# How the rows of three expert tiles reach TensorE: whole rows turned by TensorE, or blocks of 32 by 32 turned by VectorE

## The chip, the core and the metric

The kernel runs on one core of a Trainium2 chip. TensorE (PE) multiplies matrices into PSUM, VectorE (DVE) and ScalarE (ACT) do elementwise work, GpSimd (POOL) issues indirect DMAs here, and SyncE (SP) issues most of the other DMAs, one after the other. The metric is the device time of one execution in microseconds, as the median of several runs.

## The reference

A graph-attention layer over 4096 nodes is followed by a mixture of experts. The second part is the one that matters here: each row is normed, a gate picks two of eight experts for it, and each expert is a two-layer network with a GELU between.

```python
x = x + gnn(_layernorm(x), adj, ...)              # attention over 4096 nodes, 4 heads
top_w, top_i = jax.lax.top_k(xf @ Wg + bg, 2)     # xf: layer-normed rows, 4096 x 256
top_w = jax.nn.softmax(top_w, axis=-1)
for e in range(8):                                # W1[e]: 256 x 1024, W2[e]: 1024 x 256
    h = gelu(xf @ W1[e] + b1[e])
    out = out + w_dense[:, e:e + 1] * (h @ W2[e] + b2[e])
```

## The kernel before, in words

The attention takes the rows in four ranges of 1024. While a range is attended to, the rows of the range before it are finished, routed, and written with their gate weights into one list per expert in device memory (`lists`, 260 floats a row). The experts then work on tiles of 256 rows of one list. There are 17 such tiles that can be planned before the last rows are routed (9 `early`, 8 `mid`), then 8 `final` tiles, one for each expert, of 512 rows or fewer, and 2 of the kind `rest`.

The last range of the attention ends at about 777 us. From there the loop at L2027 goes over the tiles: `up` multiplies a tile with W1 and sends it through the GELU on ScalarE (L1885, L1889), `turn` brings the next tile's rows into the form that `up` needs, with the 256 features on the partitions (`xT`), and `down` multiplies with W2 (L1919). Its results are scaled by VectorE (L1932, into `o`) and added to the output by GpSimd (L1944). TensorE works in the order in which the code is written here (`order_of`), so what `turn` puts on TensorE stands between `up` of a tile and `down` of the same tile. VectorE, ScalarE and SyncE take the work in an order that the scheduler lays down at build time.

Between the parts of the first tiles, `between(n)` puts the last 1024 rows of the attention: their results are turned back (L1551), normed and summed on VectorE (L1554 to L1584, two halves of 512 rows with one Newton root of six short steps and more in each, L168 to L181), turned for the gate (L1257, copied out of PSUM by ScalarE at L1260), and routed (L1268 to L1349). The tiles share PSUM with this work: all turned pieces go through three rotating banks of the name `bank`.

A tile's rows come in one of two ways, which `fetch` (L1789) chooses by `NEAR`:

- Of the first `NEAR` tiles the whole rows are loaded by one DMA of 260 KB (`load_rows_of`, L575, into `early`; the first tile into `xr0` ahead of this stage). `turn_rows_of` (L607) turns each by four transposes of 128 by 128 on TensorE (L611, into `pt`) and two copies on ScalarE (L613), or one on ScalarE and one on VectorE (L615).
- Of the later tiles the rows are loaded in blocks (`load_blocks_of`, L583): one small DMA for the four values behind each row (`known`, L588), and eight DMAs of 32 partitions by 8 blocks by 32 floats (`xr`, L595), which put each block of 32 by 32 where it belongs in the turned tile. One VectorE instruction then turns every block in place (L1869).

After the rows, `fetch` asks for the second bias, W1 and W2 of the tile (L1804, L604, L1811). Each has two buffers, and so the DMA waits until the tile two before is done with its own. Three tiles are fetched ahead of the loop, and each pass of it fetches one more. The whole rows of tiles 2 to 6 are asked for in this prologue:

```python
        for i in range(1, NEAR):
            load_full(i)
            if i in (1, 4):
                jobs.append(fetch(*todo[len(jobs)]))
            if i in (1, 2):
                given.append(loads_of(b0 + i - 1, (residuals, large)[i - 1]))
```

Tiles are counted from 1 in the text; the code counts `i` from 0.

Of the kernel before, what the change touches and what calls it, by code (L numbers as in the profile page):

```python
# [44 lines left out]
def gat_then_moe(  # L45
# [34 lines left out]
    MID = BOTH - EARLY  # L80
    LATE = 2 * N // TT - BOTH
    SURE = 2
    NEAR = 6
    KT = -(-N // TT)
    LAG = 6

# [132 lines left out]
    def forward(apart, stack):  # L219
# [352 lines left out]
        def load_rows_of(t, i, xr):  # L572
            rows = TT
            first = entry(t, 1, i, E * LIST - WT)
            ins = nc.sync.dma_start(  # L575
                xr, lists[bass.ds(first, rows), :].rearrange("(c p) d -> p c d", p=CH)
            ).ins
            needs_of(ins, False)
# [40 lines left out]
        with ExitStack() as layer:  # L619
# [893 lines left out]
            def loads_of(b, room):  # L1513

                xb, rb = loaded("xf"), room("rb")
                nc.sync.dma_start(rb, rows_of(residual, b))
                nc.sync.dma_start(xb, rows_of(x, b))
                return xb, rb
# [270 lines left out]
        def fetch(t, i):  # L1789

            rows = rows_of_job(t, i)
            nch = -(-rows // CH)
            chosen = t is early or t is mid
            near = chosen and i + EARLY * (t is mid) < NEAR
            if near:
                xr = full_rows[i]
                known = xr[:, :, D:]
            else:
                xr = work.tile([P, DC, rows // Q, Q], F32, tag="xr", name="xr")
                known = work.tile([CH, nch, RW - D], F32, tag="known", name="known")  # L1800
                load_blocks_of(t, i, xr, known, chosen)
            e = entry(t, 0, i, E - 1)
            b2b = work.tile([CH, D], F32, tag="b2b", name="b2b")
            nc.sync.dma_start(b2b, b2[bass.ds(e, 1)].to_broadcast([CH, D]))  # L1804
            if t is early and i == 0:
                w1 = w10
            else:
                w1 = work.tile([P, DC, F], F32, tag="w1", name="w1")
                load_first(t, i, w1)
            w2 = work.tile([P, FC, D], F32, tag="w2", name="w2")  # L1810
            nc.sync.dma_start(w2, W2[bass.ds(e, 1)].rearrange("o (c p) d -> p (o c) d", p=P))  # L1811
            job = {"t": t, "i": i, "xr": xr, "known": known, "w1": w1, "w2": w2, "nch": nch, "b2b": b2b}
            job["rows"], job["near"] = rows, near
            job["last"] = t is rest and i == SURE - 1

            job["into"] = out[: N - R] if t is early or t is mid else out
            return job
# [196 lines left out]
        def load_full(i):  # L2014
            xr = work.tile([CH, 2, RW], F32, tag="early", name="early", bufs=NEAR - 1)
            load_rows_of(early, i, xr)
            full_rows.append(xr)

        for i in range(1, NEAR):
            load_full(i)  # L2020
            if i in (1, 4):
                jobs.append(fetch(*todo[len(jobs)]))
            if i in (1, 2):
                given.append(loads_of(b0 + i - 1, (residuals, large)[i - 1]))
# [61 lines left out]


    held, further, held_back, last_sums = forward(True, ctx)
    with tc.If(held(1, 1) > 0):
        further()  # L2090
        with tc.If(held(2, 1) > 0):
            with ExitStack() as again:
                held, further, rest_of_sums, _ = forward(False, again)
                with tc.If(held(1, 1) > 0):
                    further()
                for add in rest_of_sums:
                    add()
            for o in last_sums:
                nc.gpsimd.memset(o, 0.0)
# [31 lines left out]
```

## Time and profile before

| what | value |
|---|---|
| median of three runs | 1255.57 us (1255.51 to 1255.64) |
| the profiled execution's own time | 1254.18 us |
| its span, first to last instruction | 1252.5 us |
| granted TensorE clock | 0.999 |
| TensorE matmuls busy | 1237.9 us, 99% of the span |
| VectorE busy | 845.1 us, 67% |
| ScalarE busy | 448.2 us, 36% |
| DMA share from 801 to 841 us | 0.62 of the 16 engines |
| DMA share from 843 to 1000 us | 0.92 of the 16 engines |

Times within the execution are counted from the start of the span. A line of the chain of waits has the start, the duration and the piece of work that the end of the program hung on. A line of the timeline has the start, the busy time, the engine, the source line, the operation, what it wrote and read, and in brackets how long the engine stood idle before and what ended that. The DMA share is the mean busy share of the 16 DMA engines.

### The profile page before, as it was taken

To read this page: it belongs to the slowest core of one execution; us is meant where nothing else is said; L and a number is where in the kernel's file an instruction comes from. 1 tells how busy PE (TensorE), PEld (TensorE's weight loads), DVE (VectorE), ACT (ScalarE), POOL (GpSimd) and SP (SyncE) were. 2 spreads that over 40 slices of the span, in tenths; PEclk is the share of its full clock that TensorE was granted. 3 is DMA by queue.
4 is the path that set the end of the run, shared out by engine and by line. 5 is a ranking of instruction groups with operands and counts; after the bars stand their busy time and mean duration, and the time that the engine had idled before them with its cause. 6 is when DMAs were issued, how large, how long until landed. Compare 5 with 4: busy or idle time off the path is not lost.

```text
span 1252.5 us, 22714 instructions
## 1 busy us (share of the span) xinstructions
PE 1237.9 (99%) x8872; PEld 647.5 (52%) x8872; DVE 845.1 (67%) x1566; ACT 448.2 (36%) x918; POOL 241.8 (19%) x217
## 2 busy tenths in 40 slices
PE   9999999999999999999999999999999999999997
PEld 5444444332233332332324423888888876666686
DVE  7998887879999989999999996855111211111110
ACT  4332322165522375322645321533323332222322
POOL 4000000001002601006110015124432222222222
PEclk9999999999999999999999999999999999999999
DMA  6333433436533746334366422868999895455662
GB/s 216 118 119 111 164 114 102 150 121 133 187 105 102 236 114 206 103 102 153 113 159 200 128 81 91 273 169 217 229 251 252 222 230 119 106 137 112 135 163 32
DMA packets 155540, 190.22 MB, mean 152 GB/s; under 512 B 72312, under 2 KB 125680, under 8 KB 155040
## 3 DMA queue, kind: packets, MB, share of 16 engines
q1 hardware_dynamic: 133392, 145.39, 40.1%
q0 software_dynamic: 20544, 36.74, 13.3%
q10 hardware_dynamic: 1488, 6.55, 1.5%
q8 instruction: 71, 1.16, 0.4%
q14 instruction: 45, 0.37, 0.1%
HBM read 155.77 MB, written 29.74 MB: 148 GB/s over the span
## 4 chain that ended last, share of the span: by engine, by line
PE 94%; DVE 3%; issue 1%; ACT 1%; DMA 0%; POOLq 0%; SPq 0%; DVEq 0%; ACTq 0%
PE acc L1202 33%; PE po L1919 18%; PE ph L1885 17%; PE den L1211 17%; PE pr L1057 2%; DVE w L1701 2%; PE ph L1105 2%; PE ptx L1257 0%; DMA early<-lists 0%; PE acc L898 0%; PE pt L784 0%; PE ptr L1503 0%; PE po L1958 0%; PE pl L1268 0%; PE acc L748 0%
## 5 line engine op out<-in xcount | busy, mean ns | idle before, releaser
L1202 PE MATMUL acc<-w,ha 128*32 128x512 f32 x4096 | 669.9, 593 | 1.3 <-ACT u L1413 0.9
L1701 DVE SCALAR_TENSOR_TENSOR w<-er,eb,am 128x1024 f32<-128x1024 f32 x496 | 606.0, 1275 | 31.1 <-PE den L1211 30.9
L1211 PE MATMUL den<-w,unit 128*2 128x512 f32 x2048 | 467.0, 592 | 0.1
L1202 PEld LDWEIGHTS acc<-w,ha 128*32 128x32 f32 x4096 | 184.9, 110 | 292.4 <-issue 253.7
L1618 ACT ACTIVATE am<-adj 128x1024 bf16<-128x1024 int32 x124 | 130.7, 1054 | 346.2 <-DVE w L1701 211.7
L1885 PE MATMUL ph<-xT,w 128*128 128x256 f32 (+5 forms) x864 | 229.9, 423 | 0.2 <-ACT hT L1889 0.2
L1919 PE MATMUL po<-w,hT 128*128 128x256 f32 (+1 forms) x1040 | 229.7, 379 | 0.0
L1889 ACT ACTIVATE hT<-ph,bias 128x256 f32<-128x256 f32 (+5 forms) x216 | 111.1, 517 | 288.1 <-issue 186.2
L1919 PEld LDWEIGHTS po<-w,hT 128*128 128x128 f32 (+1 forms) x1040 | 195.7, 189 | 31.2 <-issue 3.1
L1885 PEld LDWEIGHTS ph<-xT,w 128*128 128x128 f32 x864 | 163.5, 190 | 59.7 <-issue 38.0
L1932 DVE SCALAR_TENSOR_TENSOR o<-po,share,b2s 128x256 f32<-128x256 f32 (+2 forms) x66 | 31.5, 478 | 210.9 <-PE po L1919 182.8
L1211 PEld LDWEIGHTS den<-w,unit 128*2 128x2 f32 x2048 | 93.7, 85 | 148.1 <-issue 139.7
L1944 POOL DMA_INDIRECT out<-o,ids x66 | 102.6, 1554 | 323.3 <-DMA out<-o,ids 141.5
L1388 POOL DMA_INDIRECT lists<-xe,at x64 | 89.3, 1395 | 267.6 <-issue 184.2
L1869 DVE STREAM_TRANSPOSE xT<-xr 128x512 f32<-128x512 f32 (+5 forms) x21 | 17.9, 851 | 70.9 <-PE ph L1885 31.2
L1057 PE MATMUL pr<-wr,xT 128*128 128x256 f32 x128 | 30.4, 381 | 0.2 <-ACT er L1151 0.2
L1907 ACT ACTIVATE b2s<-b2b,share 128x256 f32<-128x256 f32 x68 | 30.0, 499 | 0.0
L1125 POOL DMA_DIRECT2D residual<-rb x6 | 4.7, 784 | 121.2 <-DVE rb L1072 121.2
L1453 POOL DMA_DIRECT2D xf<-in_x x6 | 8.1, 1345 | 102.2 <-ACT xf L1452 102.2
L1057 PEld LDWEIGHTS pr<-wr,xT 128*128 128x128 f32 x128 | 24.1, 190 | 5.4 <-issue 0.9
L1105 PE MATMUL ph<-wall,xT 128*128 128x264 f32 x96 | 24.6, 399 | 0.0
L207 ACT ACTIVATE m<-y,off 128x256 f32<-128x256 f32 x48 | 23.7, 494 | 1.1 <-DVE off L215 0.6
(394 smaller groups left out, 616.4 us busy)
## 6 DMA issues: line engine op xcount, KB each, us to landing
adj<-in_adj SPq DMA_DIRECT2D x126, 512.0 KB
w<-in_L_ffn_W SPq DMA_DIRECT2D x54, 1024.0 KB
er<-parts ACTq DMA_DIRECT2D x3, 2048.0 KB
lists<-zeros POOLq DMA_DIRECT2D x8, 520.0 KB
residual<-rb POOLq DMA_DIRECT2D x8, 512.0 KB
rb<-residual SPq DMA_DIRECT2D x8, 512.0 KB
out<-y POOLq DMA_DIRECT2D x8, 512.0 KB
xb<-in_x SPq DMA_DIRECT2D x7, 512.0 KB
```

Of the source, the lines that this page charges most:

```text
L1057: order_of(nc.tensor.matmul(pr[:, k, :], turned[b][:, c, ts(t0 + k, P)], wr[:, c, :], start=(c == 0), stop=(c == DC - 1),))
L1105: order_of(nc.tensor.matmul(phs[t - t0], xT[:, c, ts(t, P)], wall[:, c, :], start=(c == 0), stop=(c == DC - 1),))
L1202: queue(nc.tensor.matmul(acc[half][h // 2][here : here + Q, :], ha[:, j, h * K + g * Q : h * K + (g + 1) * Q], w[half][h], start=(j == 0), ...
L1211: queue(nc.tensor.matmul(den[here : here + HB, :], unit[:, j, h, 1 - half : 1 - half + HB], w[half][h], start=(j == 0 and half == 0), stop ...
L1388: ins = nc.gpsimd.indirect_dma_start(lists, bass.IndirectOffsetOnAxis(ap=at[:, k, t : t + 1], axis=0), xe[:, t, :], None,).ins
L1618: nc.scalar.activation(am, at, AF.Relu, scale=2.0)
L1701: marks["w"] = nc.vector.scalar_tensor_tensor(wh[:, these], er[:, these, h], eb[:, j, h : h + 1], mask[:, these], op0=OP.max, op1=OP.min,).ins
L1885: order_of(nc.tensor.matmul(ph, job["w1"][:, c, ts(f, P)], xT[:, c, :], start=(c == 0), stop=(c == DC - 1),))
L1889: job["gelu"] = nc.scalar.activation(hT[:, f, :], ph, AF.Gelu, bias=job["bias"][:, f : f + 1]).ins
L1919: order_of(nc.tensor.matmul(po[:size], hT[:, f, k * CH : k * CH + size], w2[:, f, :], start=(f == 0), stop=(f == FC - 1),))
L1932: given_out.append(nc.vector.scalar_tensor_tensor(o[:size], po[:size], share[:size, k : k + 1], b2s[k][:size], op0=OP.mult, op1=OP.add,).ins)
L1944: added.append(add().ins)
```

## The change

`NEAR` goes from 6 to 3, and the number 4 in the prologue becomes `NEAR - 1`, which is 2.

```diff
-    NEAR = 6
+    NEAR = 3
...
         for i in range(1, NEAR):
             load_full(i)
-            if i in (1, 4):
+            if i in (1, NEAR - 1):
                 jobs.append(fetch(*todo[len(jobs)]))
             if i in (1, 2):
                 given.append(loads_of(b0 + i - 1, (residuals, large)[i - 1]))
```

Through `NEAR`, tiles 4, 5 and 6 are loaded by `load_blocks_of` and turned at L1869. The buffers `early` go from five to two (`bufs=NEAR - 1`). Tile 3 is now fetched after two whole-row loads instead of four.

## The prediction, made before the changed kernel had run

> **What bounds the kernel now.** I read the shares by engine first, then the chain of waits in order of time through the expert tiles, then each engine's timeline where the change lies. The page's first part and the head of the chain:
>
> ```profile
> PE 1237.9 (99%) x8872; PEld 647.5 (52%) x8872; DVE 845.1 (67%) x1566; ACT 448.2 (36%) x918; POOL 241.8 (19%) x217
> PE 94%; DVE 3%; issue 1%; ACT 1%; DMA 0%; POOLq 0%; SPq 0%; DVEq 0%; ACTq 0%
> ```
>
> TensorE sets the end. So only time that TensorE spends or loses between about 777 us and the end counts, and what it wins there arrives at the end if nothing later makes it wait. The chain where tiles 4, 5 and 6 are turned:
>
> ```profile
> 818.46 0.48 ACT xT L1260
> 818.94 0.04 issue
> 818.98 0.44 PE pt L611 x2
> ...
> 850.69 0.44 PE pt L611 x4
> 851.12 6.91 PE po L1919 x32
> ...
> 865.15 6.91 PE po L1919 x32
> 872.06 6.91 PE ph L1885 x32
> ```
>
> For tile 4 the second pair of transposes waited for a PSUM bank which ScalarE was still copying out. Tile 6 shows the transposes without the wait. Tile 7, the first loaded in blocks, has nothing between two runs of 6.91 us; from there TensorE's own list of waits is empty to 1245 us. TensorE's timeline gives the price of one turn (start, busy time):
>
> ```profile
> 818.26 0.38 PE L611 MATMUL pt<-ident,early 128*128 128x128 f32 x2
> 818.98 0.44 PE L611 MATMUL pt<-ident,early 128*128 128x128 f32 x2 [0.34 <-ACT xT L1260]
> ...
> 834.83 0.38 PE L611 MATMUL pt<-ident,early 128*128 128x128 f32 x2
> 835.45 0.44 PE L611 MATMUL pt<-ident,early 128*128 128x128 f32 x2 [0.24 <-ACT xT L1260]
> 835.72 7.07 PE L1919 MATMUL po<-w,hT 128*128 128x256 f32 x32
> ...
> 850.52 0.60 PE L611 MATMUL pt<-ident,early 128*128 128x128 f32 x4
> 850.96 7.07 PE L1919 MATMUL po<-w,hT 128*128 128x256 f32 x32
> ```
>
> The first `po` of tile 3 starts at 819.26, so the three turns hold TensorE for 1.00, 0.89 and 0.44 us.
>
> [...] L1869 writes `xT` itself in 0.71 us, while L611 needs a copy (L613). [...] a 128 B packet of `xr` held its engine 15.1 ns on average, a 1040 B packet of `early` 50.3 ns, so a byte is 2.4 times as dear in blocks. [...] the trace shows L1869 held 7.30 us at 959.37.
>
> **The change, part by part.**
>
> *Removed from TensorE*: three times four transposes. At a pitch of 0.109 us that is 1.31 us, and with the bank waits behind ScalarE, 1.00 + 0.89 + 0.44 = 2.33 us. The built order of the changed kernel has exactly these twelve gone, with `down` directly after the gate's transposes. What is late next: `down` needs a PSUM room (of the two, the earlier was given back by 808.0 us, before 818.3), its W2 (asked for at 794.4) and the first GELUs (the last ends at 818.06, and is needed 1.5 us after `down` starts). Nothing else stands there, so I take the full 2.33.
>
> *Removed from ScalarE*: six copies, 3 x 0.65 = 2 us, off the path.
>
> *Added on VectorE*: three turns of 0.71 us, 2.1 us. VectorE is full up to 826 us, so they push what is behind. The built order puts the first after a root step of the first half (806.44 to 806.60), ahead of `xe`, and moves the second half's `y` (L1563) ahead of `xe` too:
>
> ```profile
> 807.94 1.52 DVE L1584 TENSOR_SCALAR xe<-y,mv,r 128x256 f32<-128x256 f32 x4
> ```
>
> `xe` then ends at 809.46 + 0.71 + 1.22 = 811.4. TensorE wants it at 817.38, so 6.0 us cover it. The second half's `xe` has two turns and one scaling (0.48) more ahead of it: 825.50 + 1.90 = 827.4, wanted at 833.96 - 1.00, so 5.6 us. The third turn lies behind the routing step that TensorE waits for. Price: 0; without the cover, each microsecond costs one.
>
> *Moved on SyncE*: five whole-row loads become two, and 27 block loads come in: 24 DMAs more. Nine take 6.56 us of the queue (843.74 to 850.30):
>
> ```profile
> 843.74 0.37 SPq L588 DMA_DIRECT2D known<-lists  x1
> 844.30 6.00 SPq L595 DMA_DIRECT2D xr<-lists  x8
> ...
> 853.79 0.71 DVE L1869 STREAM_TRANSPOSE xT<-xr 128x512 f32<-128x512 f32 x1 [0.16 <-issue]
> ```
>
> In the built order those of tile 4 follow W2 of tile 3, which waits for `down` of tile 1 (issued 794.36). So they go out from 795.3 to 801.9, and SyncE was idle from 795.8 to 803.0. Landing took 2.3 to 4.8 us after the last issue where VectorE stood waiting (912.97, 959.37), so the blocks are there at 804.2 to 806.7, and VectorE asks at 806.6. Those of tiles 5 and 6 fall into 811.6 to 818.2 and 826.3 to 832.9, where SyncE also sat idle until 820.4 and 836.95. Behind them stand bias, W1 and W2 of the same tile: W1 of tile 4 went out at 803.9, and `up` wants it at 825.9. Price 0. Two loads that disappear stood ahead of tile 3's weights, which go out up to 2.7 us earlier, also covered.
>
> *DMA engines*: a tile in blocks is 2048 packets x 15.1 ns and 256 small ones x 9.2 ns, over 16 engines 2.1 us; in rows 256 x 50.3 ns, 0.8 us. Three tiles add 3.9 us, against 0.38 x 40 = 15 us idle from 801 to 841. Price 0.
>
> *Later on*: TensorE runs 2.33 us ahead into the stretch from 843 us where the engines are 0.92 busy. The tightest place in it is the scaling held behind a late turn: 946.55 against the next use of that room at 951.5. Of 4.9 us, 2.6 remain. Turned tiles themselves were at least 8.7 us early.
>
> **Sum.** Span 1252.5 - 2.33 = 1250.2; the profiled execution 1254.18 - 2.33 = 1251.85. It ran 1.39 us under the median, so the median becomes 1255.57 - 2.33 = 1253.2 us. That is 0.19%, just inside the 0.2% (2.5 us) that a measurement of this kernel can tell from no change.
>
> **Rivals.**
>
> *B, the bank waits come back.* Only the 1.31 us of transposes are won if the 1.0 us of waiting moves to the next user of a bank: 1254.3. For it: ScalarE still copies the gate's two turned pieces. Against: the next bank (`pl`) is asked for 6.9 us later.
>
> *C, more is won.* At 785.23 VectorE had waited 0.89 us for the whole rows of tile 2, and TensorE stood behind it. With three such loads gone from the queue around it, up to 0.9 us could come back: down to 1252.4. Against: those loads stand behind the rows of tile 2 in the same queue.
>
> *D, VectorE takes the bound.* If tile 4's blocks land late, L1869 holds `xe`, and TensorE stops at 817 us. This costs from a landing after 812.6 on, eats the gain at 814.9, and from 817.4 on shows as slower. For it: the worst tile of the trace took 15.0 us from its first block DMA to its turn (930.46 to 945.47), which would be 810.3 here, and W2 of tile 3 is in flight in front of them. Against: that was with the engines full, here they are 0.62 busy. Landing 5 us past 814.9 would give 1258.2.
>
> *E, the late stretch swallows it.* If the added packets put the turns more than 2.6 us later there, TensorE waits and part of the gain goes: about 1254.5. Against: shares of 0.59 and 0.63 at 852 and 868 us let the queue empty.
>
> **Chances and range.** The forecast 0.56, of which 0.22 lies past 2.5 us, since a turn's cost is known only to 0.1 to 0.2 us; its own range is 1252.9 to 1253.7. B 0.08, C 0.20, D 0.12 (0.11 slower by over 0.2%), E 0.04. Faster 0.22 + 0.20 = 0.42, slower 0.11, same the rest, 0.47. From 1252.3 to 1255.2 leaves out D and a little of C.
>
> **What would show it.** Right: no L611 after 805 us; `po` of tile 3 directly behind `ptx`, 1.0 us earlier; `up` of tile 6 starting at 855.8 instead of 858.1; TensorE without waits to the end; L1869 near 807, 824 and 837. Wrong: an idle time of TensorE before `ptx` at 817 or 833 put down to VectorE (D), a wait at `pl` or `ptx` for ScalarE (B), `po` waiting for L1932 after 900 us (E), or tile 2's transposes earlier than 786.2 (C).

## The result, and the profile after

The changed kernel took 1252.77 us (median of 17 runs, 1251.38 to 1257.34), the kernel before 1255.49 us in the same set (17 runs, 1253.96 to 1258.76). The ratio is 0.9983 with a 95% interval of 0.9975 to 0.9991, so 1.1 to 3.1 us less. The forecast was 1253.2 us, from 2.33 us of TensorE time.

The kernels here have execution times in two groups about 1.5 us apart (before: near 1254.0 and near 1255.5; changed: 1251.4 to 1251.8 with a mean granted clock of 0.998 to 0.999, and 1252.7 to 1253.5 with 0.997), and a median can fall in either group, so below each run also has a length out of its trace. It goes from the start of tile 2's `up` to the start of tile 6's `up` and covers all three turns. The profiled execution of the changed kernel (1253.52 us, span 1251.7 us, clock 0.997) had TensorE at half its clock for 3.4 us, from 7.8 to 11.3 us, ahead of that length; the one of before has its clock at 1.00 there. Behind the stretch, at L1148, it was 1.40 us later than before (15.32 us against 13.92). Its stage begins 1.38 us later, and the times below are shifted by that much.

| from tile 2's `up` to tile 6's `up` | before | after |
|---|---|---|
| start of `up` of tile 2 | 794.16 us | 795.54 us |
| start of `up` of tile 6 | 858.00 us | 857.05 us |
| length | 63.84 us | 61.51 us |

That is 2.33 us less, to the last digit what the three turns had held. TensorE's timeline of the kernel before has the two starts, and the gate's transposes (`ptx`) and `po` around the turn of tile 4:

```profile
794.16 2.75 PE L1885 MATMUL ph<-xT,w 128*128 128x256 f32 x12
...
817.38 1.04 PE L1257 MATMUL ptx<-ident,xe 128*128 128x128 f32 x8
...
819.26 7.07 PE L1919 MATMUL po<-w,hT 128*128 128x256 f32 x32
...
858.00 7.15 PE L1885 MATMUL ph<-xT,w 128*128 128x256 f32 x32
```

The shares by engine on the page of the changed kernel, first:

```profile
PE 1237.3 (99%) x8860; PEld 646.3 (52%) x8860; DVE 846.9 (68%) x1569; ACT 446.8 (36%) x912; POOL 241.9 (19%) x217
```

Twelve matmuls and six ScalarE instructions are gone; VectorE has three instructions and 1.8 us more. TensorE's busy time falls by only 0.6 us. Part of the gain was waiting, and the stretch at half the clock made the same matmuls longer (the four of L898 in it took 1.94 us, before 1.10), so this row could not have been the measure. The chain of waits of the changed kernel, at the places where tiles 4 and 6 had been turned (start, duration, piece):

```profile
818.93 0.87 PE ptx L1257 x8
819.80 6.91 PE po L1919 x32
...
850.06 0.11 PE pg L1277
850.17 6.91 PE po L1919 x32
```

`po` starts where the gate's work ends, without `pt` and without ScalarE in between. TensorE's timeline of the changed kernel says it again, and gives the starts:

```profile
795.54 2.75 PE L1885 MATMUL ph<-xT,w 128*128 128x256 f32 x12
...
818.76 1.04 PE L1257 MATMUL ptx<-ident,xe 128*128 128x128 f32 x8
819.64 7.07 PE L1919 MATMUL po<-w,hT 128*128 128x256 f32 x32
...
834.33 1.04 PE L1257 MATMUL ptx<-ident,xe 128*128 128x128 f32 x8
...
857.05 7.15 PE L1885 MATMUL ph<-xT,w 128*128 128x256 f32 x32
```

Before, `po` of tile 3 started 1.88 us after its `ptx` (817.38 to 819.26); here it is 0.88. VectorE's timeline of the changed kernel has the three turns and, ahead of the gate, the two `xe` that they push:

```profile
808.20 0.71 DVE L1869 STREAM_TRANSPOSE xT<-xr 128x512 f32<-128x512 f32 x1 [0.21 <-DMA b2b<-in_L_ffn_b]
...
811.10 1.38 DVE L1584 TENSOR_SCALAR xe<-y,mv,r 128x256 f32<-128x256 f32 x4
...
825.28 0.71 DVE L1869 STREAM_TRANSPOSE xT<-xr 128x512 f32<-128x512 f32 x1
...
826.67 1.38 DVE L1584 TENSOR_SCALAR xe<-y,mv,r 128x256 f32<-128x256 f32 x4
...
838.05 0.71 DVE L1869 STREAM_TRANSPOSE xT<-xr 128x512 f32<-128x512 f32 x1 [0.54 <-DMA xr<-lists]
```

The first `xe` is done at 812.48 and TensorE uses it at 818.76; the second is done at 828.05 and used at 834.33. Both times 6.28 us are to spare. The turns themselves waited at most 0.54 us for a load. SyncE issued the eight block DMAs of tile 4 from 797.38 to 803.72, and VectorE had them turned 5.2 us after the last of these.

To the end the profiled execution gives back 0.48 us: twice, in tiles 8 and 9, TensorE's weight loads waited for a GELU (0.40 us at 890.10, 0.35 us at 904.13), and its matmuls lost part of that. A second profile of the same kernel, below, has none of it.

### The profile page after: what moved, and what is told of

Same layout as the page of the kernel before. It is cut to its first block, busy times and chain, and to the rows that moved or that the text cites. A ratio compares the mean times of both kernels' runs of the same rounds, so it can differ in the third digit from the quotient of the medians.

```text
span 1251.7 us, 22777 instructions
## 1 busy us (share of the span) xinstructions
PE 1237.3 (99%) x8860; PEld 646.3 (52%) x8860; DVE 846.9 (68%) x1569; ACT 446.8 (36%) x912; POOL 241.9 (19%) x217
## 4 chain that ended last, share of the span: by engine, by line
PE 94%; DVE 3%; issue 1%; DMA 1%; ACT 1%; POOLq 0%; SPq 0%; DVEq 0%; ACTq 0%
PE acc L1202 33%; PE po L1919 18%; PE ph L1885 17%; PE den L1211 17%; PE pr L1057 2%; DVE w L1701 2%; PE ph L1105 2%; PE ptx L1257 1%; PE acc L898 1%; DMA early<-lists 0%; PE pt L784 0%; PE ptr L1503 0%; PE po L1958 0%; PE pl L1268 0%; PE po L879 0%
## 5 line engine op out<-in xcount | busy, mean ns | idle before, releaser
L1869 DVE STREAM_TRANSPOSE xT<-xr 128x512 f32<-128x512 f32 (+5 forms) x24 | 20.0, 833 | 92.5 <-DMA b2b<-in_L_ffn_b 31.9
```

## The experiments

The theory: TensorE's time in the three turns, waits included, is the whole gain, and what the change adds (24 DMAs, 6,530 packets by the page's count, three VectorE turns) is hidden. The rivals: the gain comes from loads that start earlier (C and its like); the added work costs something and the gain is net of it (D, E); the waits come back at the next bank (B). Where C would show, ahead of tile 2's `up`, the lengths of the table don't reach; the wait that it names is read further down. The expectations of two runs call the sixth `up` "tile 7's"; it is tile 6's, as in the table. All lengths in this table are from tile 2's `up` to tile 6's `up`; the ratio is to the kernel before, run on the same chip in the same set.

| run | length, us | against before | median, us | ratio, 95% interval |
|---|---|---|---|---|
| before | 63.84 | | 1254.26 to 1255.49 in four sets | |
| changed kernel | 61.51 | -2.33 | 1252.77 | 0.9975 to 0.9991 |
| changed kernel again | 61.50 | -2.34 | 1251.65 | 0.9974 to 0.9989 |
| NEAR = 5 | 63.40 | -0.44 | 1253.38 | 0.9987 to 1.0002 |
| NEAR = 4 | 62.50 | -1.34 | 1253.76 | 0.9982 to 1.0000 |
| second hunk alone | 63.84 | 0.00 | 1255.27 | 0.9996 to 1.0013 |
| no turn at all in tiles 4 to 6 | 61.51 | -2.33 | 1252.26 | 0.9973 to 0.9988 |
| block loads on top | 63.84 | 0.00 | 1254.92 | 0.9991 to 1.0009 |
| 13 turns of tile 4 | 68.52 | +4.68 | 1258.85 | 1.0021 to 1.0048 |
| before, turns in one bank | 62.51 | -1.33 | 1252.68 | 0.9978 to 0.9991 |
| changed, turns in one bank | 61.20 | -2.64 | 1251.86 | 0.9963 to 0.9983 |
| NEAR = 2 | 60.76 | -3.08 | 1250.83 | 0.9959 to 0.9980 |
| NEAR = 2, table loaded early | 59.88 | -3.96 | 1251.28 | 0.9960 to 0.9980 |
| NEAR = 1, table loaded early | 59.95 | -3.89 | 1253.66 | 0.9984 to 1.0000 |

**One turn, then two.** Only tile 6 in blocks, and then tiles 5 and 6:

```diff
-    NEAR = 6
+    NEAR = 5
```

> Only tile 6 comes in blocks and is turned by VectorE; tiles 4 and 5 stay with whole rows. Theory T (the gain is the time that the turns hold TensorE: 1.00, 0.89 and 0.44 us for tiles 4, 5 and 6; the loads and VectorE's part are hidden): 0.44 us faster than before, tile 7's up starts 0.44 us earlier behind tile 1's. Rival R (what helps is that whole-row loads leave SyncE's queue ahead of the first weights): one load of three is gone, so about a third of the whole gain, 0.8 to 0.9 us. Rival B (bank waits come back elsewhere): 0.44 us too, this tile had no such wait.

```diff
-    NEAR = 6
+    NEAR = 4
...
-            if i in (1, 4):
+            if i in (1, NEAR - 1):
```

> Tiles 5 and 6 come in blocks, tile 4 stays with whole rows. T: 0.89 + 0.44 = 1.33 us faster than before, and the wait of 0.24 us before the second pair of transposes of tile 5 is gone with them. B: only 0.44 + 0.44 = 0.88 us, the wait shows at another user of a bank. R: two thirds of the whole gain, 1.6 to 1.8 us.

The stage is 0.44 us shorter with one turn gone, 1.34 us with two and 2.33 us with three. Step by step that is 0.44, 0.90 and 0.99 us, against 0.44, 0.89 and 1.00 us that the turns of tiles 6, 5 and 4 held. Each tile brings its own turn and nothing else. The ratios go the same way (0.9995, 0.9991 and 0.9983), but the steps are smaller than their intervals; the trace decides here.

**The second hunk alone.** All turns stay on TensorE, and tile 3's bias and weights are fetched after the second whole-row load:

```diff
-            if i in (1, 4):
+            if i in (1, 2):
```

> The second hunk alone: NEAR = 6 and all turns on TensorE as before, but the fetch of tile 3 (its bias, W1 and W2) stands behind the whole rows of tile 3 instead of those of tile 5. The theory of the turns: this moves nothing on TensorE, so from the start of tile 2's `up` to that of tile 6's 63.84 us as before, and a ratio of 1.000. The rival that the gain came from earlier loads: up to 61.5 us, as in the changed kernel.

63.84 us, and a ratio of 1.0004. Earlier weights for tile 3 are worth nothing in this stage.

**Nobody turns.** The loads of before, but no turn of tiles 4 to 6 on any engine:

```diff
         else:
             prepare(job)
+            if job["t"] is early and job["i"] in (3, 4, 5):
+                return xT0
```

> Whole rows of tiles 2 to 6 are loaded as before, but tiles 4, 5 and 6 are turned by nobody: their first product takes tile 1's turned rows instead of their own. So TensorE loses the twelve transposes and ScalarE the six copies, and nothing is added on VectorE, SyncE or the DMA engines. T: the same gain as the change, 2.33 us in the trace. R: no gain, since all loads are as before. A theory in which VectorE's turns or the blocks cost part of the gain: clearly more than the change, by that part (VectorE's three turns alone are 2.1 us).

61.51 us, the length of the changed kernel, although VectorE turns nothing for these tiles and all whole rows are loaded. TensorE's timeline of this run:

```profile
795.45 2.75 PE L1887 MATMUL ph<-xT,w 128*128 128x256 f32 x12
...
856.96 7.15 PE L1887 MATMUL ph<-xT,w 128*128 128x256 f32 x32
```

So the three turns on VectorE and the other way of loading, taken together, cost nothing and bring nothing. The next run takes the loads by themselves.

**Block loads on top.** All of before, and the 27 block loads of tiles 4 to 6 besides, into buffers that nobody reads:

```diff
             if near:
                 xr = full_rows[i]
                 known = xr[:, :, D:]
+                if i in (3, 4, 5):
+                    also = work.tile([P, DC, rows // Q, Q], F32, tag="xr", name="xr")
+                    besides = work.tile([CH, nch, RW - D], F32, tag="known", name="known")
+                    load_blocks_of(t, i, also, besides, chosen)
```

> As before the change, but the blocks of tiles 4 to 6 are loaded besides their whole rows, and nobody reads them: 27 DMAs more on SyncE and 3.9 us more of all DMA engines, alone. T: no change of the time, under 0.2 us; no wait of TensorE anywhere after 858 us. Rival E (the added packets take part of the gain later on, or hold weights): slower than before by the part that they take, 0.3 us or more.

The timeline of TensorE in this run, and its window from 801 to 841 us (length, busy time of PE, PEld, DVE, ACT and POOL with counts, clock, share of the DMA engines, GB/s):

```profile
818.25 0.38 PE L611 MATMUL pt<-ident,early 128*128 128x128 f32 x2
818.98 0.44 PE L611 MATMUL pt<-ident,early 128*128 128x128 f32 x2 [0.34 <-ACT xT L1260]
```

```profile
801.00:841.00 40.00, 38.90 (x210) 33.56 (x209) 28.48 (x120) 18.40 (x39) 8.81 (x7) 1.00 0.77 187
```

The DMA engines are busy 0.77 of the time instead of 0.62. That is 0.15 x 40 = 6.0 us, and the prediction's price of a tile in blocks, three times 2.1 us, was 6.3. Yet `pt` of tile 4 stands at the same places as before to 0.01 us, and the later part of the trace is unchanged too (450.20 us from tile 2's `up` to the last `po`, in both). The loads are free here in the queue, in the DMA engines and in the full stretch after 843 us.

**The changed kernel again.**

> The changed kernel once more, for a second profile and for its time beside the kernels of this set. T: 2.33 us less between the start of tile 1's up and the start of tile 7's up than before (81.06 to 78.73 us, as in its first profile), and the median 2.3 us lower. If the two short waits of TensorE for ScalarE in tiles 8 and 9 of the first profile (0.48 us together) belong to the change, they are there again; if they were of that execution alone, they are gone.

61.50 us, and from there to the end of the last `po` nothing is lost: 447.87 us from tile 2's `up`, against 450.20 before, again -2.33. So the 0.48 us in tiles 8 and 9 belonged to that one execution; why its GELUs came late I don't know.

**How much cover VectorE has.** The changed kernel with tile 4 turned 13 times over the same buffers:

```diff
-                nc.vector.transpose(
+                for _ in range(13 if job["t"] is early and job["i"] == 3 else 1):
+                    nc.vector.transpose(
...
```

> The changed kernel with VectorE's turn of tile 4 done 13 times over the same buffers: twelve more, 12 x 0.71 = 8.5 us less what overlaps, some 7.5 to 8.5 us ahead of the rest of the second half's rows. The theory that VectorE's turns are hidden behind 6.3 us of cover gives that cover its size: VectorE is 7.5 to 8.5 us later with the second half's `xe`, so TensorE waits 1.2 to 2.2 us ahead of the second `ptx`, and the time is 1.2 to 2.2 us above the changed kernel. If the cover were larger, or VectorE had slack elsewhere, the time is that of the changed kernel; if VectorE bounded the stage at all times, it is 8 us above.

Instead of 1.2 to 2.2 us this lost 7.0 us against the changed kernel, and not ahead of `ptx`. TensorE's timeline, VectorE's last turn of tile 4, and three windows (columns as above):

```profile
825.24 0.64 PE L1268 MATMUL pl<-xT,wg 128*32 128x128 f32 x16
829.98 10.02 PE L1886 MATMUL ph<-xT,w 128*128 128x256 f32 x32 [4.10 <-DVE q L177]
```

```profile
829.22 0.70 DVE L1870 STREAM_TRANSPOSE xT<-xr 128x512 f32<-128x512 f32 x1
```

```profile
830.00:832.00 2.00, 2.00 (x5) 1.64 (x6) 1.76 (x12) 0.00 (x0) 0.00 (x0) 0.50 1.09 357
832.00:834.00 2.00, 2.00 (x7) 1.55 (x6) 1.22 (x4) 0.68 (x2) 0.00 (x0) 0.50 1.09 168
834.00:836.00 2.00, 2.00 (x7) 1.61 (x6) 0.00 (x0) 0.74 (x2) 1.57 (x1) 0.55 0.27 39
```

The expectation took the thirteen turns to stand in one block. The scheduler had laid them between other instructions, from 806.80 to 829.92, and `up` of tile 4, which could have started at 825.8, needs the last of them (the profile names VectorE's instruction directly behind it). That is a wait of 4.1 us. The clock was at half from 829.0 to 835.8 us, and TensorE worked for 5.8 us of that, so `up` and what follows took 9.97 us instead of 7.12, another 2.85. The cover of 6.3 us is therefore not confirmed by this run. It confirms only the direction, that TensorE stops when a turned tile is late enough. The second `xe` was done at 833.2, 6.6 us later than in the changed kernel, and by then TensorE was late already.

**One bank for a turn.** All four transposes into one PSUM bank and one ScalarE copy, first in the kernel before, then in the changed one, where tiles 2 and 3 are still turned by TensorE:

```diff
-            for c in range(DC):
-                pt = bank([P, TT], "pt")
...
+            pt = bank([P, DC, TT], "pt")
+            for c in range(DC):
...
+            nc.scalar.copy(xT, pt)
```

> Tiles 2 to 6 stay with whole rows and TensorE, but the four transposes of a tile go into one bank of PSUM, and one ScalarE copy of 512 columns takes them out. So the transposes stay, and the wait for a second bank goes. T: of 2.33 us of the turns, 1.01 us was waiting in tiles 4 and 5, and all of it goes here; tile 3 had a wait of 0.53 us and tile 2 of 0.34 us before the second pair, so up to 1.8 us faster than before. A theory in which the waits only move (B): 0 to 0.3 us.

> The changed kernel, with one bank for the turns of tiles 2 and 3, which it leaves to TensorE. T: these two had waits of 0.34 and 0.53 us before their second pairs, and up to 0.2 us of lost pipelining at each; 0.7 to 1.1 us faster than the changed kernel, 3.0 to 3.4 us faster than before. B: as the changed kernel.

In the kernel before this wins 1.33 us. Tile 3's turn holds TensorE 0.75 us less, tile 4's 0.56 and tile 5's 0.46. The last two, 1.02 us, are what the sum of 2.33 us counted as waits for a bank, so these waits were a cost of their own. All three together are 1.77 us; but 0.45 us is lost again in tile 3's `up`. In the changed kernel 0.75 us is won at tile 3 and the same 0.45 us lost, which leaves 0.31. TensorE's and ScalarE's timelines of the first of these two runs:

```profile
809.23 2.75 PE L1882 MATMUL ph<-xT,w 128*128 128x256 f32 x12
812.15 4.58 PE L1882 MATMUL ph<-xT,w 128*128 128x256 f32 x20 [0.18 <-ACT hT L1886]
```

```profile
810.33 1.28 ACT L1886 ACT_TABLE_LOAD   x1 [4.01 <-PE ph L1882]
```

ScalarE had done its Exp by 806.33 and stood idle for 4 us without the GELU's table. It began to load it only when TensorE's first product was there, and the three banks of `ph` filled up behind it. In the kernel before and the changed one this load runs directly behind the Exp at tile 3 (808.23 in the latter). The built programs show the difference. In all of them the table load stands directly ahead of the first GELU after the Exp. At tile 3 of before and after that GELU waits for TensorE alone, and the load ahead of it for nothing. In these two runs the GELU also waits for an earlier instruction of ScalarE itself, and then the wait for TensorE stands ahead of the load. The traces have that wait too. In the chains of the two runs a semaphore instruction of 0.02 us on ScalarE (ACTq, at 810.29 and 812.12) stands directly ahead of the load (810.33 and 812.16). At tile 3 of the changed kernel there is none, and ScalarE waits behind the load instead, 3.40 us up to the GELU at 812.92. The load takes 1.28 us at both places, and nothing beside it: in the changed kernel it starts 0.01 us after the Exp ends, and in the run with the early table, below, the GELU starts 0.02 us after the load.

**A third tile more.** Tile 3 in blocks too:

```diff
-    NEAR = 6
+    NEAR = 2
...
-        for i in range(1, NEAR):
-            load_full(i)
-            if i in (1, 4):
+        for i in range(1, 3):
+            if i < NEAR:
+                load_full(i)
+            if i in (1, 2):
```

> Tile 3 also comes in blocks and is turned by VectorE, so only tile 2 is turned by TensorE. T: the turn of tile 3 held TensorE for 1.19 us (803.76 to 804.95 in the changed kernel's trace), so 1.2 us faster than the changed kernel and 3.5 us faster than before, if VectorE's turn, which stands in the first half's first root, isn't late: it has 6.3 us of cover up to the gate's transposes. Rival D (VectorE, held by late blocks, takes the bound): TensorE idle before the gate's transposes or before up of tile 3, and less than 1.2 us, or a loss.

60.76 us, 0.75 less than the changed kernel. Tile 3's turn is gone entirely (from the start of tile 2's `up` to `po` 8.22 us instead of 9.41, so 1.19 us), and again 0.45 us is lost to the table load at tile 3's `up`. At tile 2 that load comes late in every kernel so far.

**The table early.** The same, with a GELU over one element in every partition right behind the Exp:

```diff
                 nc.scalar.activation(m, m, AF.Exp)
+                wg = small.tile([P, 1], F32, tag="wg", name="wg")
+                nc.scalar.activation(wg, m[:, 0, :1], AF.Gelu)
```

> Tile 3 in blocks too (as in the run with NEAR = 2), and behind the Exp of each half ScalarE does a GELU over one element in every partition, into a tile that nobody reads. In the run with NEAR = 2 ScalarE loaded the GELU table only when TensorE's first product of tiles 2 and 3 was there (1.28 us each, at 795.28 and 810.41), and the `up` of each took 7.35 us instead of 6.90. If that load is the reason, both fall to 6.90: from the start of tile 2's `up` to that of tile 6's 60.76 - 0.90 = 59.86 us, and the time is 0.9 us below NEAR = 2, some 4.0 us below before (ratio 0.9963 to 0.997). If the three banks of `ph` are short for another reason, such as the bias that the GELU reads, the stage stays at 60.76 us.

ScalarE's timeline of this run, and TensorE's at the same place:

```profile
810.49 1.28 ACT L1564 ACT_TABLE_LOAD   x1
811.79 0.20 ACT L1564 ACTIVATE wg<-u 128x1 f32<-128x1 f32 x1
```

```profile
810.28 7.07 PE L1887 MATMUL ph<-xT,w 128*128 128x256 f32 x32
```

Both `up` are back to 6.90 us, and the length is 59.88 us against 59.86 expected. From tile 1's `up` to the last `po` this version needs 463.08 us, before 467.28, the changed kernel 465.43 and 464.80, NEAR = 2 alone 464.09. It is the shortest that I have, by the trace. In the timed runs its shortest is 1249.56 us against 1253.60 of before, 4.0 us, and against 1250.45 of NEAR = 2 alone, 0.9 us; by medians it can't be told from NEAR = 2 alone.

**Tile 2 as well.** The same with `NEAR = 1`:

> The same with tile 2 in blocks as well (NEAR = 1), so that no tile but the first is turned by TensorE. The theory of the turns: tile 2's turn held TensorE from 785.7 to 787.26 in the run with NEAR = 2, so from tile 1's `up` to tile 2's 16.96 - 1.56 = 15.4 us, and from there 59.9 us as with NEAR = 2 and the small GELU. The rival that late blocks hold VectorE: tile 2's blocks are issued some 6 us after the whole rows were landing (VectorE asked for those at 784.5 and had them at 785.24), and the bookkeeping that reads them stands ahead of `z` and `y` on VectorE. Then `z` comes about 2 us later, the Exp and the first half's `xe` with it, and if that is over the cover of some 6.3 - 0.9 - 1.6 = 3.8 us TensorE waits ahead of the first `ptx`, or at tile 2's `up` for its turned rows. With a delay of 2 us nothing is lost and the time is 1.6 us below the other run; with one over 6 us it is no better or slower.

From tile 1's `up` to tile 2's it took 15.71 us against 16.84 in the run above, 1.13 us won where 1.56 was expected: the turn gave 1.60, and 0.48 went in front of tile 2's `up`, mostly on W1 of that tile, which the profile names as the releaser. VectorE did `z` 8.41 us after the start of tile 1's `up`; in the run above it was 8.44. So the late blocks did not hold it, and rival D does not show even here. Yet the run is slower than the one above. The loss is 240 us later, at the first tile of 512 rows. TensorE, VectorE and two windows there:

```profile
1013.33 7.07 PE L1921 MATMUL po<-w,hT 128*128 128x256 f32 x32
1022.82 15.70 PE L1887 MATMUL ph<-xT,w 128*128 128x512 f32 x32 [2.42 <-DVE xT L1871]
```

```profile
1020.50 0.48 DVE L1934 SCALAR_TENSOR_TENSOR o<-po,share,b2s 128x256 f32<-128x256 f32 x1 [2.97 <-issue]
...
1021.52 1.25 DVE L1871 STREAM_TRANSPOSE xT<-xr 128x1024 f32<-128x1024 f32 x1
```

```profile
1022.80:1026.80 4.00, 3.98 (x6) 1.67 (x7) 1.62 (x5) 0.22 (x1) 1.56 (x1) 0.57 0.55 150
1026.80:1036.00 9.20, 9.20 (x23) 4.14 (x22) 0.00 (x0) 3.90 (x6) 1.56 (x1) 1.00 1.01 245
```

In this build the turn of the next tile stands on VectorE behind the second scaling of the current one, which has to wait for the end of `po`. In the run above it stands behind the first (1018.52), and in before and after ahead of both (1011.91 and 1013.31). So `up` starts 2.58 us late (9.49 us after `po` instead of 6.91), and then TensorE runs at half the clock for 3.4 us, which costs 1.79 us: 4.37 us in all, more than was won. It is not rival D or E, but one place in VectorE's order. That the rows themselves were there is argued, not shown: their last load was issued by 1007.6 us, 13.9 us ahead of the turn, and in the run above, where the same loads went out 0.6 us earlier, the turn did not wait for them at 1018.52.

## Why the prediction was right

*Removed from TensorE.* The sum, 2.33 us with its parts 1.00, 0.89 and 0.44, came out as 2.33, with 0.99, 0.90 and 0.44 shown tile by tile by the runs with NEAR 5 and 4. Taking the bank waits as part of the gain was right (rival B is out): `po` of tile 3 starts 1.00 us earlier, no wait at `pl` or `ptx` appeared in place of the bank waits, and the one-bank run of the kernel before shows that they had been TensorE's own loss.

*Added on VectorE, priced 0.* Shown by the run in which nobody turns, the same 61.51 us, once the loads alone are known to cost nothing. The cover was given as 6.0 and 5.6 us and read as 6.28 both times. How the loss begins beyond it is not measured, since the run meant for it ran into another wait first.

*Moved on SyncE and DMA, priced 0.* Shown by the block loads on top. The places were right too. In the time of before, the loads of tile 4 went out from 795.4 to 802.3 us (predicted 795.3 to 801.9), and the three turns ran at 806.8, 823.9 and 836.7 (near 807, 824 and 837). The tail of the third set of loads was 1.4 us later than predicted, at no cost.

*Rival C* expected VectorE's wait of 0.89 us for tile 2's rows to shrink. It was 0.87 us in the changed kernel and 0.73 in its second profile. The traces that still load five whole tiles show 0.58 to 0.89 us, so no shrinking can be told from chance. The loads taken away stand behind those rows in the queue, which was the argument against. *Rival D* did not occur: the first turn waited 0.21 us. One of its sums is off, and nothing rests on it: blocks that land 5 us past 814.9 would give 1260.6 us; the 1258.2 belongs to 5 us past 812.6. *Rival E* did not occur: in the second profile TensorE has no wait from 805 us to 1250.

*The time.* The stage came out to 0.01 us. The median fell by 2.7 us in its set, where 2.33 was forecast, and with 1252.77 it lies 0.1 us below the forecast's own range, 1252.9 to 1253.7, and inside the wider one. By the shortest runs of the set the fall is 2.58 us, from 1253.96 to 1251.38. Of the 0.25 us more than the stage, the second profile has 0.15 us ahead of tile 2's `up`; the rest is not explained. It means nothing on which side of 0.2% the change landed: by the medians it is 0.22%, by the ratio 0.17%. That it is a gain at all is shown, as the interval leaves out 1.

## What to carry to other kernels

Price a removed step by what it holds the bounding engine, its waits included, read from the timeline between the neighbours that stay; the busy time alone (1.31 us here) would have missed 1.0 of 2.3 us. Before calling the added work free, measure the cover behind it and then test it in two runs: the added work with nothing removed, and the removal with nothing added. A gain at the front can be lost hundreds of microseconds later through one instruction's place in another engine's queue, so follow the end of the trace too.

## What the runs showed of the hardware

In two runs TensorE paid twice for a long wait. After a wait of 2.4 us (NEAR = 1) its clock was at half for 3.4 us, from 1022.9 to 1026.3. In a wait of 4.1 us (13 turns) it fell to half 3.1 us after TensorE had stopped and stayed there for 6.8 us, twice as long. This cost 1.79 and 2.85 us on top of the waits. The same place without a wait, in the run with NEAR = 2 and the early table, has no such stretch (13.74 us from `up` to `po` instead of 15.53, and a clock of 1.00 from 1000 to 1100 us).

The length of a wait alone does not decide it. From 220 to 320 us TensorE is idle for 0.92 us in each of five traces (before and in the changed kernel in one wait, up to 258.05 and 259.45). Before, the changed kernel and the 13 turns have a clock of 1.00 in these 100 us; NEAR = 1 and NEAR = 2 with the early table have 0.98. One stretch of 3.4 us at half the clock would give 0.983, by my estimate from the lengths above; that it lies behind this wait is not shown. The changed kernel's stretch from 7.8 us began behind a wait of 0.59 us (up to 7.34); NEAR = 2 with the early table has the same wait (up to 7.55) and a clock of 1.00 from 4 to 12 us. Between 777 and 870 us, waits of up to 0.66 us left the clock at 1.00 in the kernel before and the changed one. What tips the clock after a short wait stays open.

A table load of 1.28 us on ScalarE cost TensorE 0.45 us where it came late, though ScalarE is idle 64% of the time, because a wait of the activation behind it stood ahead of it. One activation of 0.20 us ahead of it gave that back twice.
